# Recommendation scorer on one Trainium2 core: product of the sums and pooled copy one step later, pooling nine steps behind

## The chip, the cores and the metric

The kernel runs on one core of a Trainium2 chip (trn2). The metric is the device time of one execution in microseconds, taken as the median of several runs. A profile was taken of one further execution. TensorE is called PE here (its weight loads PEld), VectorE DVE, ScalarE ACT, GpSimd POOL and SyncE SP, as in the profile.

## The reference, cut to what matters

All tensors are float32, indices int32. There are B = 16384 samples with F = 69 user fields each, and a table `emb` of 100001 rows of E = 96.

```
u  = emb[batch_user]            # B x 69 x 96: 1,130,496 gathered rows
ql = emb[batch_label[:, 0]]     # B x 96
q  = ql broadcast over the 69 fields
z  = concat(q, u, q - u, q * u)
h  = dice(z @ W1 + b1, a1)      # 64 wide; dice: p = sigmoid(x*s), (a*(1-p) + p) * x
att = (h @ W2 + b2) @ W3 + b3   # one number for each sample and field
pre = where(batch_user < 100000, u * att, 0)
pooled = einsum('gf,bfe->bge', window, pre)     # 10 groups of fields
x = concat(pooled.reshape(B, 960), ql)
h = dice(x @ Wf1 + bf1); h = dice(h @ Wf2 + bf2); return h @ Wf3 + bf3
```

## The kernel before, in words

**Tiles and steps.** The samples are cut into 32 blocks of 512. A chunk is 512 pairs of sample and field: 64 chunks of a block hold 8 samples with 64 fields each, and 5 more ("tails") hold one of the last five fields for all 512 samples. So there are 69 chunks a block, 2208 in all, and a step `i` works on the two chunks `2i` and `2i+1`: 1104 steps and one closing step.

**What one pair of chunks goes through.** Seven pieces of work, written by seven functions:

1. `fetch(i)`: POOL gathers four times 128 rows a chunk into the buffer `u` (pool `upool`, 14 buffers); PE transposes them into PSUM (`ptr`, two buffers); DVE copies them to `uT` and multiplies them by the sample's own row to `quT`.
2. `hidden(i)`: PE forms the 64 sums of both chunks in PSUM (`ph`, pool `ps_h`, two banks); ACT takes the sigmoid into `y`; DVE makes the product of the sums and the gate in two instructions (L406 and L407) and leaves it in `y`.
3. `attend_rows(b, 4)`, once for four steps: PE reduces four `y` to a band `prow`, ACT copies it to `row`.
4. `spread(b, 4)`: PE transposes the band to `patt`, DVE turns it into the weights `rw` (two instructions, L436).
5. `pool(i)`: PE multiplies the gathered rows `u` by the weights `rw` into `acc`, eight matmuls as written (one for each quarter of a chunk; the trace has two records for each); DVE copies `acc` to `pooled` (L470). `ps_acc` has one buffer.
6. `attend_tail(i, j)`: the same for a tail chunk, through `pa` and `pre`.
7. `top1`, `top2`, `top3`: the three last layers of a block, spread over ten steps after the block's end.

**A quarter of some chunks comes another way.** For 109 chunks SP, and for 136 chunks ACT, fetch one quarter row by row: 128 DMAs of 384 bytes into the SBUF tensor `ring` (four buffers for SP, three for ACT), issued at L301 with addresses loaded at L286. SP issues a chunk's 128 in a row. ACT issues 16 in each step (`scalar_rows(i)`), in its own queue between the sigmoids.

**What sets the order.** The program is recorded with `tc.manual_schedule()`: nothing reorders it. A dictionary `plan` has for each step a list of pieces, filled by `at(step, ...)`, and each engine gets its instructions in that order. [...] In step `i` the order is: rows of the band that ends at `i-3` (where `i % 4 == 2`), tails of `i-3`, spread of the band (where `i % 4 == 3`), `hidden(i-2)`, ACT's 16 row DMAs, `pool(i-7)` (`POOL_LAG = 7`), `fetch(i)`, then pieces of the last layers. So DVE's own order in a step is: weights if it is their turn, product of `i-2`, pooled copy of `i-7`, `uT` and `quT` of `i`. PE's order is: rows, spread, sums of `i-2`, pooling of `i-7`, transposes of `i`. The last sixteen steps have an order of their own.

**Buffers and who frees them.** A gather buffer `u` is freed by PE's pooling of that step. The `acc` buffer is freed by DVE's pooled copy, the `ph` bank by DVE's product, the `ptr` buffer by DVE's `quT`.

Of the kernel before, what the change touches and what calls it, by code (L numbers as in the profile page):

```python
# [11 lines left out]
F32 = mybir.dt.float32  # L12
# [7 lines left out]
B, F, E, G = 16384, 69, 96, 10  # L20
# [9 lines left out]
NS = BLK // FM  # L30
# [7 lines left out]
S_BN = float(1.0 / np.sqrt(1.0 + 1e-5))  # L38


POOL_LAG = 7

NIDS = 4

# [2 lines left out]
CLOSE = 8  # L47
# [10 lines left out]
SINGLES = SP_CHUNKS + ACT_CHUNKS  # L58
NSB = (len(SINGLES) + P - 1) // P
NSEM = 8  # L60


def chunk_of(c):

    n, k = divmod(c, NCH)
    if n == NBLK - 1 and k >= EARLY:
        k = NMAIN + k - EARLY if k < EARLY + NTAIL else k - NTAIL
    return n, k
# [47 lines left out]
def rec_kernel(  # L116
# [12 lines left out]
    nc = tc.nc  # L129
# [1 line left out]

    const = ctx.enter_context(tc.tile_pool(name="const", bufs=1))
    ipool = ctx.enter_context(tc.tile_pool(name="ipool", bufs=2))
    upool = ctx.enter_context(tc.tile_pool(name="upool", bufs=14))
    tpool = ctx.enter_context(tc.tile_pool(name="tpool", bufs=4))
    ypool = ctx.enter_context(tc.tile_pool(name="ypool", bufs=6))
    rpool = ctx.enter_context(tc.tile_pool(name="rpool", bufs=2))
    bpool = ctx.enter_context(tc.tile_pool(name="bpool", bufs=2))
    xpool = ctx.enter_context(tc.tile_pool(name="xpool", bufs=1))
# [110 lines left out]
    ps_h = ctx.enter_context(tc.tile_pool(name="ps_h", bufs=2, space=PSUM))  # L250
    ps_x = ctx.enter_context(tc.tile_pool(name="ps_x", bufs=2, space=PSUM))
    ps_acc = ctx.enter_context(tc.tile_pool(name="ps_acc", bufs=1, space=PSUM))
    ps_m = ctx.enter_context(tc.tile_pool(name="ps_m", bufs=1, space=PSUM))


# [19 lines left out]
    class Singles:  # L275

        def __init__(self, name, engine, kind, chunks, first, buffers, group):
            self.name, self.engine, self.kind, self.group = name, engine, kind, group
            self.chunks, self.first, self.buffers = chunks, first, buffers
            self.sems = [tc.alloc_semaphore(f"{name}{k}") for k in range(NSEM)]  # L280
            self.given = [0] * NSEM

# [106 lines left out]
    def hidden(i, uT, quT):  # L389

        ph = ps_h.tile([P, 512], F32, tag="h", name=f"ph{i}")
        places = [chunk_of(2 * i + j) for j in range(2)]
        sums = [ph[j * H1 : (j + 1) * H1, :] for j in range(2)]
        for (n, k), p in zip(places, sums):
            if k >= NMAIN:
                nc.tensor.matmul(p, Cq, qTs[n % 2], start=True, stop=False)
        for j, ((n, k), p) in enumerate(zip(places, sums)):
            if k < NMAIN:
                nc.tensor.matmul(p, As[n % 2][:, k // 4, :], uT[j], start=True, stop=False)  # L399
            else:  # L400
                nc.tensor.matmul(p, A, uT[j][0:E], start=False, stop=False)
        for j, p in enumerate(sums):
            nc.tensor.matmul(p, Wp, quT[:, j, :], start=False, stop=True)  # L403
        y = ypool.tile([P, 512], F32, tag="y", name=f"y{i}")
        nc.scalar.activation(y, ph, AF.Sigmoid, scale=S_DICE)  # L405
        nc.vector.scalar_tensor_tensor(y, y, na1c, ph, ALU.mult, ALU.mult)  # L406
        nc.vector.scalar_tensor_tensor(y, ph, a1c, y, ALU.mult, ALU.add)  # L407
        return y

    def attend_rows(b, n):  # L410

# [11 lines left out]
        nc.tensor.matmul(pa, vrep[j * H1 : (j + 1) * H1, :], y[j * H1 : (j + 1) * H1, :], start=True, stop=True)  # L423
        nc.vector.scalar_tensor_tensor(pres[n][:, k - NMAIN, :], pa, bb[0:E], uT[j][0:E], ALU.add, ALU.mult)  # L424

    def spread(b, n):

        row = bands.pop(b)
        pt = ps_x.tile([P, 4, n, 32], F32, tag="x", name=f"patt{b}")
        for t in range(4):  # L430
            nc.tensor.transpose(  # L431
                pt[:, t].rearrange("p k j -> p (k j)"), row[:, t * P : (t + 1) * P], ident[0 : 32 * n, 0 : 32 * n]
            )
        rw = rpool.tile([P, 16, 2, 2 * G], F32, tag="rw", name=f"rw{b}")[:, 0 : 4 * n]
        for j in range(2):
            nc.vector.scalar_tensor_tensor(  # L436
                rw[:, :, j, :],
                pt.rearrange("p t k j -> p (t k) j")[:, :, j : j + 1].to_broadcast([P, 4 * n, 2 * G]),
                bb,
                R.rearrange("p (o g) -> p o g", o=1).to_broadcast([P, 4 * n, 2 * G]),  # L440
                ALU.add,
                ALU.mult,
            )
        for k in range(n):
            rws[b + k] = rw[:, k::n]
            ys.pop(b + k)

    def pool(i):

        u, rw = us.pop(i), rws.pop(i)  # L450
        todo = [(j, *chunk_of(2 * i + j)) for j in range(2)]
        todo = [(j, n, k) for j, n, k in todo if k < NMAIN]
        if not todo:
            return
        pa = ps_acc.tile([E, 2, NS, G], F32, tag="acc", name=f"acc{i}")
        for j, n, k in todo:
            for t in range(4):
                read_rows(
                    nc.tensor.matmul,
                    pa[:, j, 2 * t : 2 * t + 2, :].rearrange("e n g -> e (n g)"),  # L460
                    u,
                    2 * i + j,
                    t,
                    rw[:, t, j, :],
                    start=True,
                    stop=True,
                )
        if len(todo) == 2:
            _, n, k = todo[0]
            nc.vector.tensor_copy(  # L470
                pooled[n][:, :, k * NS : (k + 2) * NS].rearrange("e g s -> e s g"),
                pa.rearrange("e j s g -> e (j s) g"),
            )
        else:
            j, n, k = todo[0]
            nc.vector.tensor_copy(
                pooled[n][:, :, k * NS : (k + 1) * NS].rearrange("e g s -> e s g"), pa[:, j]
            )
# [58 lines left out]
        nc.vector.tensor_scalar(r, p3, bf3c[0:1], None, ALU.add)  # L537
        nc.sync.dma_start(out=out[B - P :].rearrange("p o -> o p"), in_=r)

    pooled, pres, x1s, x2s, qs, us, hs, ys, bands, rws, p1s = ({} for _ in range(11))  # L540

    def top_steps(n, cols):

# [14 lines left out]
    def rows_of(b, n):  # L558
        return lambda: attend_rows(b, n)

    def spread_of(b, n):
        return lambda: spread(b, n)

    def pool_of(k):
        return lambda: pool(k)

    def hidden_of(k):
        return lambda: ys.__setitem__(k, hidden(k, *hs[k]))

    def tails_of(k):  # L570
        def work():
            uT = hs.pop(k)[0]
            for j in range(2):
                if chunk_of(2 * k + j)[1] >= NMAIN:
                    attend_tail(k, j, ys[k], uT)

        return work

    def fetch_of(k, between=()):
        def work():  # L580
            for j in range(2):
                n = chunk_of(2 * k + j)[0]
                if n not in pooled:
                    pooled[n] = bpool.tile([E, G, BLK], F32, tag="pooled", name=f"pooled{n}")
                    pres[n] = xpool.tile([E, NTAIL, BLK], F32, tag="pre", name=f"pre{n}")
            u, uT, quT = fetch(k, lambda: [w() for w in between])
            us[k], hs[k] = u, (uT, quT)

        return work
# [4 lines left out]
    def at(step, *work):  # L594
        plan.setdefault(step, []).extend(work)
# [19 lines left out]
    def scalar_rows(i):  # L615

        for s, start, stop in turn.get(i, []):
            by_scalar.fetch(s, start, stop)

    c = NPAIR - CLOSE  # L620
    for i in range(c):
        if i >= 3 and (i - 3) % 4 == 3:
            at(i, rows_of(i - 6, 4))
        if i >= 3:
            at(i, tails_of(i - 3))
        if i >= 4 and (i - 4) % 4 == 3:
            at(i, spread_of(i - 7, 4))
        if i >= 2:
            at(i, hidden_of(i - 2))
        at(i, lambda i=i: scalar_rows(i))  # L630
        if i < c - CLOSE:
            if i >= POOL_LAG:
                at(i, pool_of(i - POOL_LAG))
        else:

            for k in {0: (-15, -14), 1: (-13,), 3: (-12, -11), 4: (-10, -9), 7: (-8, -7)}.get(i - c + 8, ()):
                at(i, pool_of(c + k))
        at(i, fetch_of(i))

    at(c, pool_of(c - 6), pool_of(c - 5), tails_of(c - 3), hidden_of(c - 2), fetch_of(c))  # L640
# [8 lines left out]
    for n in range(NBLK):  # L649
        first, end = n * NCH // 2, ((n + 1) * NCH - 1) // 2  # L650
        if n > 0:
            if n % NIDS == 1:
                at(max(0, first - 50), lambda n=n: load_ids(n))
            at(first - 14, lambda n=n: qs.__setitem__(n, head_gather(n)))
            at(first - 11, lambda n=n: head_turn(n, qs.pop(n)))
            at(first - 9, lambda n=n: head_rows(n))
        if n < NBLK - 2:
            for s, work in enumerate(top_steps(n, slice(0, BLK))):
                at(end + POOL_LAG + 4 + s, work)
        elif n == NBLK - 2:  # L660
            for s, work in enumerate(top_steps(n, slice(0, BLK))):
                at(end + POOL_LAG + s // 2, work)
    for f in range(NTAIL):
        at(2 + 2 * f, lambda f=f: tail_weights(f))

# [89 lines left out]
```

## Time and profile before

| | |
|---|---|
| time, median of 3 runs | 13698.38 us (13690.1 to 13716.8) |
| the profiled execution's own time | 13662.58 us, its span 13660.8 us |
| mean granted TensorE clock | 0.723 of full speed |
| PE busy | 9255.3 us, 68% of the span |
| POOL busy | 8237.3 us, 60% |
| DVE busy | 5106.9 us, 37% |
| ACT busy, its DMA issuing not counted | 992.1 us, 7% |
| row DMAs issued by ACT, by SP | 17408 and 13952 |
| gathers issued by POOL | 8715 |

The span is the time from the first instruction of the profiled execution to its last. Busy time of an engine is the union of its instructions; issuing a DMA and waiting for a semaphore don't count for ACT and SP, so an ACT that is full of issues looks idle. A group of section 5 of the page gives busy time, mean duration of one in nanoseconds, and the engine's idle time just before its instructions; "issue" and "remote" there mean that the profile shows no instruction that ended the wait. Some matmul records are missing from the trace, and then the wait for them shows as "remote". The profiled execution lies 0.26% below the median of the runs.

### The profile page before, as it was taken

The page shows a single profiled execution, that of the slowest core. Times are in us where ns is not written, and L with a number is a line of the kernel's source. Part 1 is how long each engine was busy: PE and PEld are TensorE (multiplying, and loading weights), DVE is VectorE, ACT ScalarE, POOL GpSimd, SP SyncE. Part 2 cuts the span into 40 slices and gives each one's busy share as a digit, 9 for nine tenths or more (in the row PEclk, how much of TensorE's full clock was granted, in tenths as well). Part 3 has the DMA queues.
Part 4 walks back from the last instruction along what each step waited for, and adds up shares of the span by engine and source line. Part 5 has one row for each costly group of instructions (what it writes and reads, how often), then busy time and mean ns, then how long its engine had stood idle before and what let it go on. Part 6 is the DMA issues. An engine that isn't in the chain of part 4 may idle for free.

```text
span 13660.8 us, 171082 instructions
## 1 busy us (share of the span) xinstructions
PE 9255.3 (68%) x41797; PEld 4797.0 (35%) x41797; DVE 5106.9 (37%) x8639; ACT 992.1 (7%) x1657; POOL 8237.3 (60%) x8721
## 2 busy tenths in 40 slices
PE   3667766667666776666776666666677666667667
PEld 2333333333333333333333333333333333333334
DVE  3333333333333333333433333333333333333333
ACT  0000000000000000000000000000000000000001
POOL 5665666565565656666666666665665666666664
PEclk7667777767766777777777777676777777777777
DMA  1111111111111111111111111111111111111111
GB/s 38 34 34 33 35 34 34 33 36 33 33 34 32 36 33 33 33 33 35 34 33 33 33 35 33 33 33 33 36 34 33 34 33 35 34 34 34 33 33 23
DMA packets 344459, 458.45 MB, mean 34 GB/s; under 512 B 202354, under 2 KB 202866, under 8 KB 343330
## 3 DMA queue, kind: packets, MB, share of 16 engines
q0 software_dynamic: 278880, 428.92, 15.8%
q1 hardware_dynamic: 29762, 11.82, 0.4%
q10 hardware_dynamic: 34816, 6.75, 0.3%
q8 instruction: 336, 5.51, 0.2%
q14 instruction: 665, 5.45, 0.1%
HBM read 446.74 MB, written 0.07 MB: 33 GB/s over the span
## 4 chain that ended last, share of the span: by engine, by line
PE 28%; issue 25%; ACTq 21%; another core or an unknown queue 14%; DVE 10%; ACT 2%; POOL 1%; DMA 0%; POOLq 0%
ACTq L301 18%; PE acc L325 6%; PE ptr L325 5%; PE ph L399 4%; PE p L502 4%; PE ph L403 4%; ACTq L286 2%; DVE uT L376 2%; DVE quT L379 2%; PE prow L414 2%; DVE y L406 2%; DVE y L407 2%; ACT y L405 1%; DVE pooled L470 1%
## 5 line engine op out<-in xcount | busy, mean ns | idle before, releaser
L266 POOL DMA_INDIRECT u<-in_rows,ids x8587 | 8115.1, 945 | 5284.9 <-issue 2284.1
L325 PE MATMUL acc<-rw,u 128*96 128x20 f32 x15930 | 2014.5, 272 | 1908.8 <-issue 1280.6
L325 PEld LDWEIGHTS acc<-rw,u 128*96 128x96 f32 x15930 | 1897.3, 205 | 2981.6 <-issue 2047.5
L406 DVE SCALAR_TENSOR_TENSOR y<-y,na1c,ph 128x512 f32<-128x512 f32 x1104 | 822.7, 745 | 4219.3 <-issue 2329.2
L325 PE MATMUL ptr<-ident,u 128*96 128x128 f32 x8587 | 1706.4, 350 | 718.5 <-issue 526.8
L376 DVE COPY uT<-ptr 96x512 f32<-96x512 f32 x2208 | 1485.5, 673 | 794.1 <-remote 619.1
L403 PE MATMUL ph<-quT,wn 96*64 96x512 f32 x4416 | 1611.4, 720 | 202.7 <-issue 196.4
L399 PE MATMUL ph<-uT,A 128*64 128x512 f32 x4096 | 1645.1, 830 | 82.0 <-issue 78.5
L325 PEld LDWEIGHTS ptr<-ident,u 128*96 128x96 f32 x8587 | 1284.6, 170 | 937.9 <-issue 701.2
L470 DVE COPY pooled<-acc 96x160 f32<-96x160 f32 x1008 | 424.7, 421 | 2693.5 <-remote 2166.1
L379 DVE TENSOR_TENSOR quT<-ptr,qT 96x512 f32<-96x512 f32 x2048 | 1378.9, 673 | 0.0
L405 ACT ACTIVATE y<-ph 128x512 f32<-128x512 f32 x1104 | 658.9, 597 | 8332.7 <-remote 3222.0
L403 PEld LDWEIGHTS ph<-quT,wn 96*64 96x64 f32 x4416 | 447.0, 175 | 1277.5 <-issue 1275.0
L407 DVE SCALAR_TENSOR_TENSOR y<-ph,wn,y 128x512 f32<-128x512 f32 x1104 | 829.1, 751 | 39.0
L414 PE MATMUL prow<-y,v 128*32 128x512 f32 x2208 | 645.9, 840 | 249.1 <-DVE y L407 133.0
L502 PE MATMUL p<-pooled,wf 96*100 96x512 f32 (+1 forms) x1400 | 701.0, 634 | 65.7 <-issue 61.6
L399 PEld LDWEIGHTS ph<-uT,A 128*64 128x64 f32 x4096 | 281.5, 170 | 753.7 <-issue 750.9
L502 PE MATMUL p<-pre,V 96*100 96x512 f32 (+1 forms) x700 | 423.9, 750 | 156.2 <-issue 107.4
L431 PE MATMUL patt<-ident,row 128*128 128x128 f32 x1108 | 257.0, 367 | 387.2 <-issue 205.8
L502 PEld LDWEIGHTS p<-pooled,wf 96*100 96x100 f32 x1400 | 249.4, 191 | 424.6 <-issue 424.0
L423 PE MATMUL pa<-y,vrep 64*96 64x512 f32 x320 | 189.8, 973 | 268.7 <-DVE pre L424 152.0
L416 ACT COPY row<-prow 128x512 f32<-128x512 f32 (+1 forms) x277 | 162.0, 585 | 2890.0 <-remote 1120.7
(72 smaller groups left out, 2729.4 us busy)
## 6 DMA issues: line engine op xcount, KB each, us to landing
ring<-in_rows ACTq DMA_DIRECT2D x17408, 0.4 KB
ring<-in_rows SPq DMA_DIRECT2D x13952, 0.4 KB
u<-in_rows,ids POOLq DMA_INDIRECT x8587
ids<-in_idx SPq DMA_DIRECT2D x8, 560.0 KB
q<-in_emb,ids POOLq DMA_INDIRECT x128
wf<-in_far SPq DMA_DIRECT2D x1, 1209.0 KB
wn<-in_near SPq DMA_DIRECT2D x1, 236.0 KB
ids<-in_idx SPq DMA_DIRECT2D x1, 140.0 KB
```

Source lines behind the costliest of these rows:

```text
L266: nc.gpsimd.indirect_dma_start(out=dst, out_offset=None, in_=table, in_offset=bass.IndirectOffsetOnAxis(ap=index, axis=0),)
L301: d = self.engine.dma_start(out=ring[r : r + 1, b], in_=row_bytes[:, bass.ds(self.values[r], ROW_BYTES)]).then_inc(self.sems[k], 16)
L325: ins = op(out, ring[:, at[0]].bitcast(F32) if at else u[:, 4 * (c % 2) + t, :], other, **how)
L376: nc.vector.tensor_copy(uT[j][0:E], ptr)
L379: nc.vector.tensor_tensor(quT[:, j, :].rearrange("e (s f) -> e s f", f=FM), ptr.rearrange("e (s f) -> e s f", f=FM), by_field(q[:, k * NS ...
L399: nc.tensor.matmul(p, As[n % 2][:, k // 4, :], uT[j], start=True, stop=False)
L403: nc.tensor.matmul(p, Wp, quT[:, j, :], start=False, stop=True)
L405: nc.scalar.activation(y, ph, AF.Sigmoid, scale=S_DICE)
L406: nc.vector.scalar_tensor_tensor(y, y, na1c, ph, ALU.mult, ALU.mult)
L407: nc.vector.scalar_tensor_tensor(y, ph, a1c, y, ALU.mult, ALU.add)
L414: nc.tensor.matmul(pr[32 * k : 32 * (k + 1), :], v2, ys[b + k], start=True, stop=True)
L502: nc.tensor.matmul(p1, w[:, h * DH : (h + 1) * DH], x, start=(k == 0), stop=(k == KTOP - 1))
```

## The change

`hidden` is cut into its sums with the sigmoid (`sums_of`) and DVE's product (`product`), `pool` into PE's matmuls (`pool_sums`) and DVE's copy (`pool_copy`), `spread` into PE's transposes (`turn_band`) and DVE's weights (`weigh`). In the main loop, which now ends sixteen steps before the last one's place (`e`), the DVE halves stand one step after the PE halves: the product of `i-3` instead of `i-2`, the copy of `i-10` beside the sums of `i-9`. `POOL_LAG` goes from 7 to 9. The one `acc` tile holds three sets of pooled sums side by side[...], set `i % 3` in turn. `upool` has 17 buffers instead of 14, `ypool` 7 instead of 6; to make room in SBUF the software DMA's scratch is set to 4096 bytes a partition. In the main loop the tails stand a step later, and the rows and the spread are put as the diff shows. The steps that lead to the end are written out anew, and the last layers of the last but one block start a step later than the new lag alone would have it.

```diff
-POOL_LAG = 7
+POOL_LAG = 9
+RING_BYTES = 4096
-    upool = ctx.enter_context(tc.tile_pool(name="upool", bufs=14))
+    upool = ctx.enter_context(tc.tile_pool(name="upool", bufs=17))
-    ypool = ctx.enter_context(tc.tile_pool(name="ypool", bufs=6))
+    ypool = ctx.enter_context(tc.tile_pool(name="ypool", bufs=7))
+    acc = ps_acc.tile([E, 3, 2, NS, G], F32, tag="acc", name="acc")
...
         nc.scalar.activation(y, ph, AF.Sigmoid, scale=S_DICE)
+        gates[i] = ph
+        ys[i] = y
+
+    def product(i):
+
+        ph, y = gates.pop(i), ys[i]
         nc.vector.scalar_tensor_tensor(y, y, na1c, ph, ALU.mult, ALU.mult)
         nc.vector.scalar_tensor_tensor(y, ph, a1c, y, ALU.mult, ALU.add)
-        return y
...
-        pa = ps_acc.tile([E, 2, NS, G], F32, tag="acc", name=f"acc{i}")
+        pa = acc[:, i % 3]
...
+        accs[i] = pa, todo
+
+    def pool_copy(i):
+
+        if i not in accs:
+            return
+        pa, todo = accs.pop(i)
...
     c = NPAIR - CLOSE
-    for i in range(c):
-        if i >= 3 and (i - 3) % 4 == 3:
-            at(i, rows_of(i - 6, 4))
-        if i >= 3:
-            at(i, tails_of(i - 3))
-        if i >= 4 and (i - 4) % 4 == 3:
-            at(i, spread_of(i - 7, 4))
-        if i >= 2:
-            at(i, hidden_of(i - 2))
-        at(i, lambda i=i: scalar_rows(i))
-        if i < c - CLOSE:
-            if i >= POOL_LAG:
-                at(i, pool_of(i - POOL_LAG))
-        else:
...
+    e = c - CLOSE
+    for i in range(e):
+        if i >= 7 and i % 4 == 3 and i < e - 1:
+            at(i, rows_of(i - 7, 4))
+        if i >= 4:
+            at(i, tails_of(i - 4))
+        if i >= 8 and i % 4 == 0:
+            at(i, lambda b=i - 8: turn_band(b, 4))
+        if i >= 2:
+            at(i, sums_of(i - 2))
+        at(i, lambda i=i: scalar_rows(i))
+        pools = [] if i < POOL_LAG else [i - POOL_LAG]
+        if i == e - 2:
+            pools.append(i - POOL_LAG + 1)
+        elif i == e - 1:
+            pools = [i - POOL_LAG + 1]
+        at(i, *[lambda k=k: pool_sums(k) for k in pools])
+        if i >= 3:
+            at(i, product_of(i - 3))
+        at(i, *[lambda k=k: pool_copy(k) for k in ([] if i <= POOL_LAG else [i - POOL_LAG - 1, i - POOL_LAG][: 1 + (i == e - 1)])])
...
+        at(i, fetch_of(i))
+        if i >= 8 and i % 4 == 0:
+            at(i, lambda b=i - 8: weigh(b, 4))
...
+    for i in range(e, c):
...
+        at(i, hidden_of(i - 2), lambda i=i: scalar_rows(i))
+        for k in {0: (-16, -15), 1: (-14,), 2: (-13,), 3: (-12, -11), 4: (-10, -9), 7: (-8, -7)}.get(i - e, ()):
+            at(i, pool_of(c + k))
         at(i, fetch_of(i))
...
-                at(end + POOL_LAG + s // 2, work)
+                at(end + POOL_LAG + 1 + s // 2, work)
...
-    nc = bacc.Bacc("TRN2", target_bir_lowering=False, num_devices=1)
+    nc = bacc.Bacc("TRN2", target_bir_lowering=False, num_devices=1, dynamic_dma_scratch_size=RING_BYTES)
```

More of the change, by code (lines that the diff above doesn't have):

```diff
@@ L424, in attend_tail, with turn_band @@
         nc.vector.scalar_tensor_tensor(pres[n][:, k - NMAIN, :], pa, bb[0:E], uT[j][0:E], ALU.add, ALU.mult)
-    def spread(b, n):
+    def turn_band(b, n):
         row = bands.pop(b)
@@ L433, in spread, with weigh @@
             )
+        turned[b] = pt
+    def weigh(b, n):
+        pt = turned.pop(b)
         rw = rpool.tile([P, 16, 2, 2 * G], F32, tag="rw", name=f"rw{b}")[:, 0 : 4 * n]
@@ L446, in spread, with pool_sums @@
             ys.pop(b + k)
-    def pool(i):
+    def pool_sums(i):
         u, rw = us.pop(i), rws.pop(i)
@@ L538, in top3_last @@
         nc.sync.dma_start(out=out[B - P :].rearrange("p o -> o p"), in_=r)
-    pooled, pres, x1s, x2s, qs, us, hs, ys, bands, rws, p1s = ({} for _ in range(11))
+    pooled, pres, x1s, x2s, qs, us, hs, ys, bands, rws, p1s, gates, turned, accs = ({} for _ in range(14))
     def top_steps(n, cols):
@@ L561, in spread_of, with work, sums_of, product_of @@
     def spread_of(b, n):
-        return lambda: spread(b, n)
+        def work():
+            turn_band(b, n)
+            weigh(b, n)
+        return work
     def pool_of(k):
-        return lambda: pool(k)
+        def work():
+            pool_sums(k)
+            pool_copy(k)
+        return work
     def hidden_of(k):
-        return lambda: ys.__setitem__(k, hidden(k, *hs[k]))
+        def work():
+            hidden(k, *hs[k])
+            product(k)
+        return work
+    def sums_of(k):
+        return lambda: hidden(k, *hs[k])
+    def product_of(k):
+        return lambda: product(k)
     def tails_of(k):
@@ L620, in rec_kernel @@
     c = NPAIR - CLOSE
-    for i in range(c):
-        if i >= 3 and (i - 3) % 4 == 3:
+    e = c - CLOSE
[18 more added lines that the diff above has]
+        at(i, *[lambda k=k: pool_copy(k) for k in ([] if i <= POOL_LAG else [i - POOL_LAG - 1, i - POOL_LAG][: 1 + (i == e - 1)])])
+        if i == e - 2:
+            at(i, rows_of(c - 16, 4))
+        elif i == e - 1:
+            at(i, lambda: turn_band(c - 16, 4))
+        at(i, fetch_of(i))
+        if i >= 8 and i % 4 == 0:
+            at(i, lambda b=i - 8: weigh(b, 4))
+        elif i == e - 1:
+            at(i, lambda: weigh(c - 16, 4))
+    at(e, product_of(e - 3), lambda: pool_copy(e - POOL_LAG), tails_of(e - 4))
+    for i in range(e, c):
+        if (i - 3) % 4 == 3:
             at(i, rows_of(i - 6, 4))
-        if i >= 3:
-            at(i, tails_of(i - 3))
-        if i >= 4 and (i - 4) % 4 == 3:
+        at(i, tails_of(i - 3))
+        if (i - 4) % 4 == 3:
             at(i, spread_of(i - 7, 4))
-        if i >= 2:
-            at(i, hidden_of(i - 2))
-        at(i, lambda i=i: scalar_rows(i))
-        if i < c - CLOSE:
-            if i >= POOL_LAG:
-                at(i, pool_of(i - POOL_LAG))
-        else:
-            for k in {0: (-15, -14), 1: (-13,), 3: (-12, -11), 4: (-10, -9), 7: (-8, -7)}.get(i - c + 8, ()):
-                at(i, pool_of(c + k))
+        at(i, hidden_of(i - 2), lambda i=i: scalar_rows(i))
+        for k in {0: (-16, -15), 1: (-14,), 2: (-13,), 3: (-12, -11), 4: (-10, -9), 7: (-8, -7)}.get(i - e, ()):
+            at(i, pool_of(c + k))
         at(i, fetch_of(i))
```

## The prediction

> **What bounds the kernel now.** I read the busy shares first, then the groups with their idle time, then the timeline of a few steps, then the clock by windows. Section 1 of the page:
>
> ```profile
> span 13660.8 us, 171082 instructions
> ...
> PE 9255.3 (68%) x41797; PEld 4797.0 (35%) x41797; DVE 5106.9 (37%) x8639; ACT 992.1 (7%) x1657; POOL 8237.3 (60%) x8721
> ```
>
> No engine is full: a step is 12.37 us (13660.8 / 1104), PE is busy for 8.4 of it. So something makes them wait for each other. Section 5 says where (after the bar: busy us, mean ns, idle before):
>
> ```profile
> L266 POOL DMA_INDIRECT u<-in_rows,ids x8587 | 8115.1, 945 | 5284.9 <-issue 2284.1
> L325 PE MATMUL acc<-rw,u 128*96 128x20 f32 x15930 | 2014.5, 272 | 1908.8 <-issue 1280.6
> ...
> L406 DVE SCALAR_TENSOR_TENSOR y<-y,na1c,ph 128x512 f32<-128x512 f32 x1104 | 822.7, 745 | 4219.3 <-issue 2329.2
> L325 PE MATMUL ptr<-ident,u 128*96 128x128 f32 x8587 | 1706.4, 350 | 718.5 <-issue 526.8
> ...
> L470 DVE COPY pooled<-acc 96x160 f32<-96x160 f32 x1008 | 424.7, 421 | 2693.5 <-remote 2166.1
> ```
>
> PE's idle time stands mostly before `acc`, DVE's before the product (L406) and the copy (L470). The timeline shows the link between them:
>
> ```profile
> 6239.41 10.26 ACTq L301 DMA_DIRECT2D ring<-in_rows  x16
> ...
> 6247.48 1.03 PE L403 MATMUL ph<-quT,wn 96*64 96x512 f32 x4
> ...
> 6249.77 0.60 ACT L405 ACTIVATE y<-ph 128x512 f32<-128x512 f32 x1 [12.04 <-PE ph L403]
> 6249.84 10.46 ACTq L301 DMA_DIRECT2D ring<-in_rows  x16
> 6250.40 0.75 DVE L406 SCALAR_TENSOR_TENSOR y<-y,na1c,ph 128x512 f32<-128x512 f32 x1 [8.45 <-ACT y L405]
> ...
> 6251.18 0.75 DVE L407 SCALAR_TENSOR_TENSOR y<-ph,wn,y 128x512 f32<-128x512 f32 x1
> 6251.85 0.41 DVE L470 COPY pooled<-acc 96x160 f32<-96x160 f32 x1
> ...
> 6252.32 1.77 PE L325 MATMUL acc<-rw,u 128*96 128x20 f32 x16 [3.81 <-issue]
> ```
>
> PE ends its sums at 6248.5 and stands still for 3.81 us. It needs the one `acc` buffer, which the copy frees at 6252.26. The copy stands behind the product, the product waits for the sigmoid, and the sigmoid stands in ACT's queue behind sixteen row DMAs (6239.41 + 10.26 = 6249.67; sigmoid at 6249.77). So ACT's issuing stops PE through DVE's queue. In other steps it is the reverse: ACT is done with its DMAs and waits for PE's sums. Going through all 1104 sigmoids, 53% start within 0.3 us of the end of ACT's earlier work, and 30% come over 2 us after it. PE and ACT take turns in holding each other up.
>
> The clock makes it worse (columns: busy of PE, PEld, DVE, ACT, POOL, then the granted clock):
>
> ```profile
> 6180.00:6190.00 10.00, 10.00 (x52) 5.20 (x50) 4.14 (x7) 0.60 (x1) 5.97 (x7) 1.00 0.15 30
> 6340.00:6350.00 10.00, 1.33 (x5) 0.51 (x5) 1.82 (x3) 0.60 (x1) 7.56 (x8) 0.50 0.21 40
> ```
>
> [...]
>
> Gathers do not bound: the first `uT` copy of a step starts 76 us or more after its gather was issued (99% of steps). POOL has filled the 14 buffers and waits for PE.
>
> [...] the clock's records are 1.0 or 0.5 only, in pieces that are multiples of 3.41 us, 0.723 in the mean. [...] The trace shows 278880 packets for 8715 gathers, 32 each[...].
>
> **The change, part by part.** As built, both programs have the same 25933 matmuls, 8636 DVE operations, 8715 gathers and 31374 DMAs of ACT and SP; PE gets 70 more pure wait instructions, a few us at most. So only order and waits move.
>
> *Product one step later.* In step i DVE does the product of i-3. Its sigmoid was queued a step earlier. In the built program, PE's transposes of i wait for `quT` of i-1 as before, but that stands behind the product of i-4, no longer i-3. Removed: most of the 718.5 us before `ptr`.
>
> *Copy one step later, three sets.* The pooling of i waits for the copy that DVE does in step i-1, as before; it is not three sets of freedom[...]. But that copy stands behind the product of i-4 instead of i-3. The weights of a band are now made a step before their first use; before, PE's `acc` waited for them some 500 us. Removed: most of the 1908.8 us before `acc`.
>
> *New wait.* With two `ph` banks and the product a step later, PE's sums of i-2 wait for the product of i-4, done by DVE in step i-1. Behind them in PE's queue stand the pooling of i-9 and the transposes of i; ACT waits for those sums. Bounds: nothing where ACT is ahead, and where ACT is late up to all that was removed. `patt` still waits for ACT's band copy of the step before (387.2 us now); a PE that runs further ahead waits longer there, once in four steps.
>
> *Gather buffers and lag.* A buffer lives 9 steps instead of 7, and there are 17: POOL may lead PE by 8 steps instead of 7. POOL's order is unchanged. Its own time is 8715 x (0.945 + 0.30) = about 10,890 us, so it has some 2770 us to spare. Rows in `ring` are freed two steps later; ACT's buffer is rewritten 14 steps after its transposes and read by the pooling 9 after them instead of 7, so ACT gets no wait. SP's refill starts two steps later, with over 20 steps to spare. Cost nothing; without that cover it would be SP's 128 issues, about 100 us a chunk.
>
> *Descriptor scratch.* Nothing in the trace of before prices it. [...] I take 0. From the other side, it decides nothing until a gather costs 1.57 us instead of 1.25 (13661 / 8715).
>
> *Ends.* First poolings two steps later, sixteen last steps rearranged: plus or minus 20 us; I take 0.
>
> **The sum.** ACT is the engine to count. Its DMA pieces add up over the trace to about 9600 us (0.55 us each), the address loads to 544 x 2.16 = 1175, what else is not under DMAs to 300: 11,075. So it is idle for about 2585 us, 1960 of them before sigmoids. How much of this goes? For each sigmoid that waited I took the smaller of ACT's wait and PE's idle time before `acc` and `ptr` since the sigmoid before, and since the one before that: 630 and 1120 us in all. These are waits that PE would not have caused had it not stood still itself. The change moves the limit by one step, so I take 1000. A less interrupted PE has a higher clock: 0.75 for 0.723 takes 3.6% off 9255 us, 330, half of it where PE is the late one: 155. Against it: next to a gather in progress ACT's issues are 0.59 us apart, with none 0.39. With POOL at 86% instead of 80% that is 0.011 x 17408 = 190, of which 110 where ACT is the late one. Sum: 13,662 - 1000 - 155 + 110 = 12,617. The median of the runs is 0.26% above the profiled execution: 12,650.
>
> **The rivals.**
>
> *A, as summed (0.52):* 12,650, itself from 12,250 to 13,150.
>
> *B, decoupled fully (0.22).* PE always has a step in hand and stays at the full clock; ACT sets the pace with POOL nearly full behind it: 11,075 + 0.035 x 17408 (issues at 0.585 us) = 11,680, with some 200 us at band copies and ends 11,900. For it: with the clock at 1.00 (6230 to 6240 us) a step's sums came 7.7 us after the last ones. Against: `patt` and the last layers still tie PE and DVE to the end of ACT's queue.
>
> *C, the wait only changes its name (0.14).* It stands before `ph` and `patt` instead of `acc`: only the 500 us at the weights go, and a third of that shows: 13,500. For it: the same sigmoid still precedes all. Some of this case lies within 0.2%.
>
> *D, slower (0.12): the clock.* If PE's waits gather into fewer, longer ones (at `patt`, up to one batch of ACT's DMAs, 8 to 10 us, every fourth step), more windows fall to half clock. At 0.5 throughout PE alone needs 9255 x 0.723 / 0.5 = 13,380, with 1000 us of waits left 14,400. It decides from a mean clock of about 0.58 on: 9255 x 0.723 / 0.58 = 11,540, and the 2160 us of PE's idle time that stand neither before `acc` nor `ptr` fill the rest. Against it: fewer waits in all.
>
> **How the numbers follow.** A measurement tells about 0.2% from no change (27 us). Faster: A, B and three quarters of C, 0.84; same: a quarter of C, 0.04; slower 0.12. The range leaves out D and the lower part of B: 11,850 to 13,720. A's own is 12,250 to 13,150.
>
> **What would show it.** Right: the idle time before `acc` falls from 1908.8 to under 800 us and before `ptr` from 718.5 to under 400; a new group of waits before `ph`, under 600; the mean clock at 0.74 or more; the product no longer starts 0.03 us after its sigmoid but finds it done. POOL's idle time falls with the span. Wrong: as much idle time before `ph` and `patt` as was taken away (C), a clock under 0.6 (D), a gather group with mean over 945 ns or new gaps between gathers (the scratch), ACT idle under 500 us (B).

## The result and the profile after

The changed kernel takes 13684.62 us (median of 12 runs, 13673.53 to 13723.87), the kernel before 13698.64 us (12 runs). The ratio is 0.9994, with a 95% interval from 0.9983 to 1.0004: no change that a measurement can tell. The forecast was 12,650 us. One thing has to be known to read what follows: in some of the later groups of runs (a group is run together on one chip) the kernel before took 13,507 to 13,657 us, near the 13,699 on record, in others 10,928 to 10,947 us, and two chips had both; so each run below is set against the kernel before of its own group. I call the first kind **stalled** and the second **free**, for a reason that the traces show. The result itself is stalled.

The page of the changed kernel, sections 1 and 5 (after the bar: busy us, mean ns of one, idle us before and what ended most of it):

```profile
span 13682.6 us, 171148 instructions
...
PE 9106.3 (67%) x41797; PEld 4711.6 (34%) x41797; DVE 5074.9 (37%) x8639; ACT 990.6 (7%) x1657; POOL 8225.3 (60%) x8721
...
L268 POOL DMA_INDIRECT u<-in_rows,ids x8587 | 8103.5, 944 | 5290.9 <-issue 2228.3
L327 PE MATMUL acc<-rw,u 128*96 128x20 f32 x15930 | 1972.9, 269 | 1685.7 <-issue 1088.5
L489 DVE COPY pooled<-acc 96x160 f32<-96x160 f32 x1008 | 429.0, 426 | 6575.4 <-remote 4728.2
...
L327 PE MATMUL ptr<-ident,u 128*96 128x128 f32 x8587 | 1655.6, 341 | 866.1 <-issue 659.3
...
L414 DVE SCALAR_TENSOR_TENSOR y<-y,na1c,ph 128x512 f32<-128x512 f32 x1104 | 810.3, 734 | 177.1 <-ACT y L407 97.0
```

The change did what it says on DVE: the product waited 4219.3 us before, now 177.1. But DVE then waits at the pooled copy (2693.5 before, 6575.4 now). PE's idle time hardly moved: before `acc` 1908.8 to 1685.7, before `ptr` 718.5 to 866.1. And POOL's row is the same to 6 us in its idle time.

That row leads to the cause. In both traces POOL's gathers come as strings, 1.249 us from one to the next, and between strings there is a stop, at nine steps in ten. Before: 979 stops over 0.6 us, median 2.35 us, 2962 us in all. After: 978 stops, median 2.39 us, 2970 us in all. For the kernel before, 8715 x 1.249 = 10,885 us of gathers and 2962 - 979 x 0.30 = 2668 us that the stops add (0.30 us is the gap between two gathers of a string) give 13,553; its last gather ends at 13,563 us of 13,661. Such a sum comes out for any engine; that each gather counts in full, stops or not, is shown by e15 below. A string is one step's gathers, 7 or 8 of them, in 850 of 978 cases before and in 849 of 977 after: three more gather buffers did not make it longer.

What happens in a string and at its end is seen in the timeline of the changed kernel (start, duration, engine; in brackets the idle time before). The usual case:

```profile
6384.47 1.53 PE L327 MATMUL acc<-rw,u 128*96 128x20 f32 x16
...
6385.85 1.06 PE L327 MATMUL ptr<-ident,u 128*96 128x128 f32 x8
...
6387.75 1.03 PE L405 MATMUL ph<-quT,wn 96*64 96x512 f32 x4
...
6388.87 0.94 POOL L268 DMA_INDIRECT u<-in_rows,ids  x1 [0.30 <-issue]
6391.82 0.42 DVE L489 COPY pooled<-acc 96x160 f32<-96x160 f32 x1 [7.74 <-remote]
6392.06 0.94 POOL L268 DMA_INDIRECT u<-in_rows,ids  x1 [2.24 <-remote]
6392.10 0.66 DVE L378 COPY uT<-ptr 96x512 f32<-96x512 f32 x1
```

PE has pooled by 6386.00, transposed by 6386.91 and summed by 6388.78, and the string's last gather ends at 6389.81. Yet DVE, with nothing else to do for 7.74 us, copies the pooled sums only at 6391.82 and the transposes at 6392.10, and POOL goes on at 6392.06. Nobody acts on PE's finished work until 2 us after the string.

Counts over the whole trace say the same. 11,358 of PE's instructions in it raise a semaphore, a counter that the other engines' instructions wait for. In e17, the kernel before in a free group, 98% of these instructions are followed by a recorded increment within 0.1 us (median 14 ns). In the trace of the changed kernel only 18% are (median 3.2 us; 9% of the increments have no record, so this is a lower bound). Of the recorded increments 81% fall between the end of a string and the restart after it, where only 19% of the raising instructions end. The first of them comes 2.03 us after the string's end in the median, and POOL restarts 0.02 us after one of them, while the last pooling had ended 6.4 us before. The kernel before shows the same (17% within 0.1 us, 80% between string and restart, 2.01 us, pooling 6.2 us earlier).

The rarer case is a PE that crawls itself:

```profile
6634.23 0.32 PE L327 MATMUL acc<-rw,u 128*96 128x20 f32 x1 [1.09 <-issue]
...
6635.68 0.32 PE L327 MATMUL acc<-rw,u 128*96 128x20 f32 x1 [1.14 <-issue]
...
6636.94 0.95 POOL L268 DMA_INDIRECT u<-in_rows,ids  x1 [0.30 <-issue]
6637.79 0.19 PE L327 MATMUL acc<-rw,u 128*96 128x20 f32 x1 [1.79 <-issue]
...
6639.20 0.19 PE L327 MATMUL acc<-rw,u 128*96 128x20 f32 x1 [1.23 <-issue]
...
6639.93 0.80 PE L327 MATMUL acc<-rw,u 128*96 128x20 f32 x4 [0.54 <-issue]
...
6641.01 0.94 POOL L268 DMA_INDIRECT u<-in_rows,ids  x1 [3.12 <-PE ptr L327]
```

Pooling matmuls of one step come here one at a time, 0.7 to 2.1 us apart, though the profile shows nothing that they wait for. The last four follow 2 us after the string's last gather ended (6637.89), and POOL restarts 0.28 us after them. Only 13% of the 978 restarts follow the last pooling within 0.5 us. Of PE's 1695 us of idle time before pooling matmuls, those on `ring` included, 1401 us stand before the first one of a step and 294 us between them.

So POOL waits for PE, as the prediction said, but mostly for word of work that PE has already done. Most of the `acc` group's idle time, "issue" included, stands where a step's pooling has to wait for DVE, and crawl between the matmuls is the smaller part. DVE hears from PE mostly once a string, with the old order of its own work as with the new (80% and 81% of the recorded increments). This fits a change that gained nothing, but no run changed when PE's word arrives.

### The profile page after: what moved, and what is told of

It reads as the page before. It is cut to its first block, busy times and chain, and to the rows that moved or that the text cites. A ratio compares the mean times of both kernels' runs of the same rounds, so it can differ in the third digit from the quotient of the medians.

```text
span 13682.6 us, 171148 instructions
## 1 busy us (share of the span) xinstructions
PE 9106.3 (67%) x41797; PEld 4711.6 (34%) x41797; DVE 5074.9 (37%) x8639; ACT 990.6 (7%) x1657; POOL 8225.3 (60%) x8721
## 4 chain that ended last, share of the span: by engine, by line
PE 37%; issue 20%; another core or an unknown queue 18%; ACTq 12%; DVE 10%; POOL 2%; ACT 1%; DMA 0%; POOLq 0%
ACTq L303 10%; PE acc L327 8%; PE ph L401 6%; PE ptr L327 6%; PE ph L405 5%; PE p L521 5%; DVE uT L378 3%; DVE quT L381 2%; POOL u L268 2%; PE prow L421 2%; DVE y L415 1%; DVE y L414 1%; ACTq L288 1%; PE pa L430 1%
## 5 line engine op out<-in xcount | busy, mean ns | idle before, releaser
L327 PE MATMUL acc<-rw,u 128*96 128x20 f32 x15930 | 1972.9, 269 | 1685.7 <-issue 1088.5
L489 DVE COPY pooled<-acc 96x160 f32<-96x160 f32 x1008 | 429.0, 426 | 6575.4 <-remote 4728.2
L327 PEld LDWEIGHTS acc<-rw,u 128*96 128x96 f32 x15930 | 1853.6, 201 | 2757.0 <-issue 1954.3
L327 PE MATMUL ptr<-ident,u 128*96 128x128 f32 x8587 | 1655.6, 341 | 866.1 <-issue 659.3
L405 PE MATMUL ph<-quT,wn 96*64 96x512 f32 x4416 | 1625.1, 727 | 195.2 <-issue 189.6
L401 PE MATMUL ph<-uT,A 128*64 128x512 f32 x4096 | 1637.7, 830 | 156.9 <-issue 106.2
L327 PEld LDWEIGHTS ptr<-ident,u 128*96 128x96 f32 x8587 | 1250.6, 166 | 1082.2 <-issue 864.1
L414 DVE SCALAR_TENSOR_TENSOR y<-y,na1c,ph 128x512 f32<-128x512 f32 x1104 | 810.3, 734 | 177.1 <-ACT y L407 97.0
L438 PE MATMUL patt<-ident,row 128*128 128x128 f32 x1108 | 259.5, 375 | 641.4 <-issue 274.9
L421 PE MATMUL prow<-y,v 128*32 128x512 f32 x2208 | 540.7, 851 | 115.0 <-issue 95.6
L438 PEld LDWEIGHTS patt<-ident,row 128*128 128x128 f32 x1108 | 185.1, 194 | 775.8 <-issue 554.0
L430 PE MATMUL pa<-y,vrep 64*96 64x512 f32 x320 | 231.3, 895 | 203.2 <-DVE pre L431 127.6
```

The source lines that it names most:

```text
L327: ins = op(out, ring[:, at[0]].bitcast(F32) if at else u[:, 4 * (c % 2) + t, :], other, **how)
L421: nc.tensor.matmul(pr[32 * k : 32 * (k + 1), :], v2, ys[b + k], start=True, stop=True)
```

## The experiments

Theories: **G**, gathers set the pace; **A**, ACT's string of row transfers sets it, as the prediction counted; **P**, PE at its clock; **R**, in the stalled groups the time follows the number of instructions and of transfers that complete, an assumption of the author's from the crawl and the missing records (counted under "What is settled, what is open"). All kernels are the changed one with an edit, but for e17. The texts written before the runs speak of two kinds of chip; the runs corrected that, chips 3 and 10 were seen in both conditions. e5, e9, e12, e14, e16 and e18 are several executions each, the others one; within a group the executions of the kernel before lie within 0.6% of each other.

### Gathers, ACT's rows, all rows, PE's work (e1 to e4; a free group, kernel before 10,946.5 us)

```
e1:  -                else:
     +                elif (j, t) != (0, 0):     # one gather less per step
e2:  ACT_CHUNKS = []
e3:  ACT_CHUNKS = []; SP_CHUNKS = [17]
e4:  - nc.tensor.matmul(p, Wp, quT[:, j, :], start=False, stop=True)
```

> The changed kernel with one gather of 128 rows per step left out: tile 0 of a step's first chunk is not fetched, its readers read tile 1's rows instead, so the output differs; all other work is there. Theory G (POOL's string of gathers sets the pace: n gathers at 1.25 us and about 2.2 us of release per step): 1104 x 1.25 = 1,380 us less, about 12,300 us. Theory A (ACT's string of row transfers sets it, as the prediction counted): ACT issues the same transfers; at most the share of them that ran beside the missing gather becomes quicker, about 1/8 of (0.61 - 0.44) us x 17,408 = 370 us less, about 13,300 us. Theory P (TensorE at its granted clock): no change, about 13,680 us.

> The changed kernel with ACT's 17,408 row transfers taken out; their 136 chunk tiles are fetched by 136 more gathers on POOL. Theory G: 136 x 1.25 = 170 us more, about 13,850 us. Theory A: ACT is left with sigmoids and copies, some 1,500 us of work, so the time falls to the next bound, between 11,000 us (POOL's 8,851 gathers at 1.245 us) and 12,500 us. Theory P: no change, 13,680 us.

> The changed kernel with the row transfers of both ACT and SP taken out (one chunk is left on SP); 244 more gathers on POOL do their work. Theory G: 244 x 1.25 = 305 us more, about 13,990 us. Theory A: as without ACT's rows, 11,000 to 12,600 us. If the two strings of row transfers slow the gathers or the release of POOL (the 2.2 us per step), this run is faster than the one in which only ACT's are out by more than SP's 108 added gathers cost it (135 us).

> The changed kernel without the 4,416 matmuls that add the second product to the sums (ph from quT); the output differs, every transfer and every other instruction stays. Theory P (TensorE sets the pace): its 1,611 us of busy time go, about 12,100 us. Theory G: TensorE releases POOL earlier by what it saves only if it is itself late; between no change (13,680) and 12,900 us. Theory A: no change, 13,680 us.

Measured: e1 9602.81 us, e2 11,116.58, e3 11,227.22, e4 10,930.76. Without 1104 gathers the time falls by 1344 us, 1.22 each; with 136 more it rises by 170, 1.25 each; with 244 more by 281, 1.15 each. 17,408 row transfers less on ACT, or 4416 matmuls less on PE, bring nothing. In these traces POOL has no stop over 0.6 us at all. For the free groups G stands, A and P fall. e2 and e4 were not run in a stalled group. The absolute figures of the expectations were for a stalled group.

### The change itself (e5, stalled; e9, free)

The edit is the change.

> The changed kernel as it is, beside the kernel before on one chip. In the group of four looks the kernel before took 10,946 us where the runs on record have 13,699 us, and in them POOL never stopped between gathers (8,715 x 1.25 = 10,894 us). Theory G2 (that chip runs both kernels at POOL's own pace of one gather per 1.25 us): here, if this chip is of that kind, both kernels take about 10,945 us and the ratio is 1.00 within 0.002, since the change neither adds nor removes a gather. If this chip is of the other kind, both take about 13,690 us and the ratio is again 0.999. Theory L (the change removes waits that count only where POOL has reserve to give): on the quick kind of chip the lead of three more buffers shows as a gain, at most the 50 us that 10,946 us has over 8,715 gathers. Against both: a difference over 1%.

> The changed kernel as it is, on the chip of the three looks before it. On a chip of the quick kind (the kernel before at 10,946 us): POOL never stops, 8,715 x 1.25 = 10,894 us; the change can give back only what lies around that, so a ratio between 0.995 and 1.001. On a chip of the slow kind: as before, between 0.998 and 1.001 by theory R, since the number of instructions and of completions is the same in both kernels.

Measured: e5 13,500.68 us against 13,510.80, ratio 0.9992 (0.9985 to 0.9999); e9 10,937.86 against 10,934.39, ratio 1.0004 (0.9995 to 1.0013). Neither condition gains: in e5 the interval leaves 1.00 by a hair, far inside what counts here as no change.

### All rows and a gather out again, and idle memsets (e6 to e8, free)

```
e7:  + filler = const.tile([P, 1], F32, name="filler")
     ... after each quT:                 for _ in range(8):  nc.vector.memset(filler, 0.0)
     ... after the product's second op:  for _ in range(16): nc.vector.memset(filler, 0.0)
```

> The same kernel as e3 (no row transfers by ACT and SP but those of one chunk; 244 more gathers), for a chip on which the kernel before takes about 13,500 to 13,700 us. On that kind of chip five sixths of the records of the gathers' completions are missing from the trace (some 2,700 of 17,400 for each of their eight semaphores), and matmuls, row transfers and VectorE's operations that wait for nothing come at multiples of 0.7 us while gathers run. Theory R (there [...]time follows the number of instructions; 63,500 of 171,100 go here): POOL's own pace becomes the bound, about 11,230 us. Theory G (gathers alone hold the others up, 2.2 us a step): 244 x 1.25 = 305 us more than 13,500 to 13,700. Theory A (ACT's own string of transfers): 11,200 to 12,600 us. On a chip of the quick kind: 11,230 us by all.

> The changed kernel with 32 VectorE memsets of one element per partition added to each step, 35,328 in all, that nothing reads; VectorE is idle for more than half of the time. Theory R, on a chip of the slow kind: a fifth more instructions, so up to a fifth more of the time, between 14,300 and 16,000 us. Theories G and A: VectorE gets some 35,328 x 0.06 = 2,100 us more of work beside its 5,100 in 13,500: no change, at most 150 us for products that come later. On a chip of the quick kind: POOL stays the bound, 10,930 to 11,000 us by all.

> The same kernel as e1 (one gather of 128 rows per step left out), for a chip of the slow kind. Theory G (n gathers at 1.25 us and 2.2 us of release per step): 1,380 us less than the kernel before. Theory R: the instructions are nearly the same (1,104 of 171,100 less) but an eighth of the gathers' completions goes: between 300 and 1,700 us less. Theory A: at most 370 us less. On a chip of the quick kind: about 9,600 us as in e1.

Measured, kernel before 10,934.39 us: e6 11,233.00, e7 10,989.28, e8 9583.96, as expected for a free group. They could not tell R from the others; 35,328 memsets cost 55 us there.

### Idle memsets for a stalled group (e10, e11 free; e13 stalled)

The edit is that of e7.

> The kernel of e7 (35,328 idle memsets on VectorE), sent for a chip on which the kernel before takes 13,500 to 13,700 us. Theory R[...]: a fifth more instructions, between 14,300 and 16,000 us. Theories G (gathers alone) and A (ACT's string of transfers): no change, at most 150 us. On a chip of the quick kind: about 10,990 us as in e7.

> The kernel of e7 and e10 (35,328 idle memsets on VectorE) once more, for a chip on which the kernel before takes 13,500 to 13,700 us. Theory R: between 14,300 and 16,000 us. Theories G and A: no change, at most 150 us. On a chip of the quick kind: about 10,990 us.

> The kernel of e7 (35,328 idle memsets on VectorE), for a chip on which the kernel before takes 13,500 to 13,700 us. Theory R: between 14,300 and 16,000 us. Theories G and A: no change, at most 150 us. On a chip of the quick kind: about 10,990 us as in e7.

Measured: e10 10,987.31 us against 10,928.05 and e11 10,993.05 against 10,929.92; both groups were free, so they add nothing to e7. e13: 14,223.10 against 13,529.23, 694 us more, 20 ns for each memset that nothing reads. Section 5 of its page:

```profile
L268 POOL DMA_INDIRECT u<-in_rows,ids x8587 | 8103.9, 944 | 5793.0 <-issue 2207.0
L365 DVE MEMSET filler<- 128x1 f32 x35328 | 2084.4, 59 | 5632.4 <-DVE filler L365 3366.5
```

The second row shows memsets that wait on their own predecessor, 3366.5 us of it (in e7 the row has 2018.7 us of idle time in all, none of it in gaps over 0.15 us): DVE crawls too. POOL's stops come to 3481 us, against 2781 in e5: the 700 us are there. By G alone and by A at most 150 us should have been lost, so instructions do cost something as such; R had the sign but its 14,300 to 16,000 us was too high.

### No rows, one gather less, for a stalled group (e14, e15)

The edits are those of e3 and e1; kernel before 13,657.44 us.

> The kernel of e3 (no row transfers but those of one chunk; 244 more gathers), for a chip of the slow kind (kernel before 13,500 to 13,700 us). Theory R: 63,500 of 171,100 instructions go; at the 20 ns that an idle memset cost there that alone is 1,250 us[...], so between 11,230 us (POOL's own pace, 8,959 x 1.25 and ends) and 12,300 us. Theory G: 305 us more than the kernel before. Theory A: 11,230 to 12,600 us. On a chip of the quick kind: 11,230 us, a ratio of 1.027.

> The kernel of e1 (one gather of 128 rows per step left out), for a chip of the slow kind. Theory G: 1,380 us less than the kernel before. Theory R: an eighth of the gathers' completions goes, 300 to 1,700 us less. Theory A: at most 370 us less. On a chip of the quick kind: about 9,600 us.

Measured: e14 13,382.43 us, ratio 0.9797 (0.9781 to 0.9814); e15 12,232.24 us. A falls here too: with no rows at all on ACT it wanted 12,600 us or less. R in its strong form falls with it: 37% of the instructions are gone and the time is 2% less. What stays of R is small: a gather less per step saves 1425 us, 1.29 each (G: 1380), so the 244 gathers that e14 has more cost about 315, and its rows saved 275 + 315 = 590 us, 19 ns each, the price of a memset in e13. In e14 POOL still makes 610 stops, 2271 us in all; in e15 991, 2904 us. The stops stay when the rows are gone; with the rows, and more with the memsets, they come to more in all (2781 us in e5, 3481 in e13). Two limits: R had allowed 300 to 1700 us for e15, so e15 alone does not tell G from a form of R that counts the gathers' completions; and P was not tested by a stalled run. The kept trace speaks against P. In the kernel before, ten steps in a row that carry a block's last layers (50 or more of their matmul records) keep PE busy for 96 us, ten that carry none for 82 us, and yet they take 123.5 and 129.2 us; in the changed kernel it is 96 and 80 us, 122.4 and 129.1.

### More rows on SP (e12, e16, e18; all stalled)

```
- SP_CHUNKS = [2 * (10 * s + 8) + 1 for s in range(109)]
+ SP_CHUNKS = [2 * (6 * s + 8) + 1 for s in range(181)]
```

> The changed kernel with 72 more chunk tiles fetched row by row by SP (181 chunks, one in 6 steps, where it has 109, one in 10) and 72 gathers fewer on POOL. On a chip of the quick kind (kernel before about 10,930 us), where POOL never stops: 72 x 1.25 = 90 us less, a ratio of 0.992, unless SP's strings of 128 rows at 0.32 us become late (41 us and the loads of offsets per 6 steps of 9.9 us), then slower. On a chip of the slow kind (13,500 to 13,700 us): theory G 90 us less or a little more; theory A no change, ACT's string is the same; theory R 72 x 128 = 9,216 more transfers, with their instructions some 18,900 (11%) more, so 300 to 1,500 us more.

> The kernel of e12 (72 more chunk tiles fetched row by row by SP, 72 gathers fewer), for an occasion on which the kernel before takes about 10,930 us: 72 x 1.25 = 90 us less, a ratio of 0.992; it would be the quickest of all kernels here with complete work. If SP's strings come late (41 us of rows and the loads of offsets per 6 steps of 9.9 us), it is slower. On an occasion with 13,500 to 13,700 us for the kernel before: 1.16 as in e12.

> The kernel of e12 and e16 (72 more chunk tiles fetched row by row by SP, 72 gathers fewer). On an occasion on which the kernel before takes about 10,930 us: 72 x 1.25 = 90 us less, a ratio of 0.992, or slower if SP's strings come late. On one with 13,500 to 13,700 us: 1.16 as before.

Measured ratios: 1.1595 (1.1563 to 1.1628), 1.1589 (1.1555 to 1.1622), 1.1519 (1.1491 to 1.1548). That is more than any theory said. The chain of e12's page and its group of transposes that read the ring name the place:

```profile
SPq 61%; issue 37%; PE 1%; DVE 0%; another core or an unknown queue 0%; DMA 0%; ACT 0%; ACTq 0%
...
L327 PE MATMUL ptr<-ident,ring 128*96 128x128 f32 x317 | 118.9, 375 | 4035.9 <-DMA ring<-in_rows 3938.7
```

SP's queue is full: 23,168 rows at 0.67 us (mean of the spacings under 3 us, here and below) are 15,520 of 15,822 us. In the free trace e9 its rows come 0.386 us apart, in the stalled trace of before 0.804. The expectation had priced a row at 0.32 us; in the stalled groups it takes twice that and turns SP into the bound. Whether the move gains in a free group was not seen.

### The kernel before in a free group (e17)

> The kernel before itself, for its trace on an occasion on which it takes about 10,930 us. If the change did what the prediction says and POOL hides it, PE's idle time before acc is several hundred us here and DVE's product waits for the sigmoid (over 500 us), against 14.6 and 32.2 us in e9. If those waits came from the stalls alone, both are as small here as in e9. On an occasion with 13,500 to 13,700 us it repeats the profile on record: about 1,900 us before acc.

Measured: 10,929.90 us, as its neighbour. Its section 5 beside that of e9, first the kernel before, then the changed one:

```profile
L266 POOL DMA_INDIRECT u<-in_rows,ids x8587 | 8104.2, 944 | 2619.7 <-issue 2413.5
L325 PE MATMUL ptr<-ident,u 128*96 128x128 f32 x8587 | 2003.9, 333 | 1963.0 <-DMA u<-in_rows,ids 1914.0
L406 DVE SCALAR_TENSOR_TENSOR y<-y,na1c,ph 128x512 f32<-128x512 f32 x1104 | 824.6, 747 | 3371.0 <-ACT y L405 3311.6
...
L325 PE MATMUL acc<-rw,u 128*96 128x20 f32 x15930 | 1801.7, 259 | 43.0 <-DVE rw L436 31.2
...
L470 DVE COPY pooled<-acc 96x160 f32<-96x160 f32 x1008 | 419.2, 416 | 115.9 <-PE acc L325 115.7
```

```profile
L268 POOL DMA_INDIRECT u<-in_rows,ids x8587 | 8113.2, 945 | 2619.2 <-issue 2431.0
L327 PE MATMUL ptr<-ident,u 128*96 128x128 f32 x8587 | 1979.3, 333 | 1892.1 <-DMA u<-in_rows,ids 1869.4
...
L327 PE MATMUL acc<-rw,u 128*96 128x20 f32 x15930 | 1808.3, 259 | 14.6 <-DVE rw L448 8.1
L489 DVE COPY pooled<-acc 96x160 f32<-96x160 f32 x1008 | 430.3, 427 | 2826.2 <-PE acc L327 2772.4
...
L414 DVE SCALAR_TENSOR_TENSOR y<-y,na1c,ph 128x512 f32<-128x512 f32 x1104 | 810.7, 734 | 32.2 <-ACT y L407 32.2
```

Of the 1908.8 us before `acc` 43.0 are left in the very same program, and of the 1280.6 us "issue" nothing. So nearly all of that idle time came with the stalls. Of the two forecasts each is half right: the wait before `acc` is as small as in e9, DVE's wait for the sigmoid is not. PE's real wait is before `ptr`, and a gather's landing ends it: POOL's idle time is 8714 gaps of 0.30 us, nothing else. DVE's wait moves from product to copy here as well, and it costs and saves nothing.

### What is settled, what is open

Settled: in the free groups POOL's gathers set the time, 1.249 us each, without stops. In the stalled ones a gather left out counts in full as well (1.29 us, e15), and stops come on top, at nine steps in ten in the result's two traces, at 610 of 1104 in e14. The change alters neither the gathers nor the stops.

Open: what holds PE's increments back while gathers run, what makes single instructions crawl, and why a string is one step long. The stalled traces also lack most records of the gathers' completions: each of their eight semaphores has 2613 to 2746 records in the kernel before, and 17,254 to 17,341 in e9, for the same 8715 gathers. Engines that crawl, increments that come late and records that are missing are seen together here; no run shows that the one causes the other.

## Why the prediction was wrong

**The step that failed** is "Gathers do not bound" with "so it has some 2770 us to spare". The 10,890 us were right (10,885 measured). The 2770 us beside them were read as a reserve, since the transposes came 76 us after their gathers and POOL waited for PE. They were 979 stops, 2.35 us in the median, one after each of POOL's own strings, until word of PE's work came through. With a reserve, a gather less a step should save nothing; it saved 1425 us in the stalled e15 and 1344 in the free e1.

**"ACT is the engine to count"** fell with it. The sum took 0.55 us for a row issue as ACT's price; it is 0.345 us between rows in e17. ACT's rows could go altogether at no gain in a free group (e2), and in a stalled one ACT's and SP's together were worth 590 us, not the pace (e14).

**"Removed: most of the 1908.8 us before acc", "most of the 718.5 us before ptr".** 1685.7 and 866.1 us stayed. The timeline shown in the prediction, with 3.81 us before `acc`, was read as a queue through product and sigmoid; but its sigmoid (6249.77) also starts 0.24 us after POOL's restart from a stop of 2.29 us (6249.53), so it fits late word from PE as well. The free trace of the same program has 43.0 us in all. One instance was taken for the group. So the term of 1000 us was 0. The wait of `acc` for the weights, put at some 500 us and expected to go, is 274.5 us before by the trace (PE's waits for `rw`) and 504.0 after.

**The clock**: 0.75 was forecast, 0.72 came (0.723 before), so the 155 us were 0 too. The two stretches shown in the prediction are near the ends of a wide range: in the trace of before, the 117 stretches of 10 us in which PE is busy for 99% or more have a clock of 0.79 in the mean, the 121 with PE busy for under 30% one of 0.61. From one piece of 3.41 us to the next the tie is closer: all 756 pieces that follow one with PE busy for under 30% have 0.5, the 1554 that follow one with 95% or more have 0.895 in the mean. And PE's time does not go fully with the clock, as the 155 us and D's 13,380 us assume: a matmul of `quT` takes 594 ns at 1.0 and 1060 at 0.5, a transpose 276 and 421, a pooling matmul 240 and 325. **ACT's pace beside gathers**, 110 us lost, had no POOL speed-up to arise from.

**What was right.** The product no longer follows its sigmoid by 0.03 us; the median is 4.34 us. The wait before `ph` stays small, 156.9 and 195.2 us for its two groups (82.0 and 202.7 before) against the 600 us allowed for a new one. The longer wait at `patt` came, 387.2 to 641.4 us. The gathers keep their 944 ns (945 before), and no cost of the smaller scratch shows. Three sets in `acc` gave no freedom, as said: in neither trace does a pooling matmul run during any of the 1040 pooled copies.

**The rivals.** C ("the wait only changes its name") comes nearest with its 13,500 us, and the name did change on DVE; but its place was to be `ph` and `patt`, and the time was kept by POOL's strings and stops, not by ACT. B and D did not come. D's 2160 us of PE idle time are 1778 in the trace (13,660.8 - 9255.3 - 1908.8 - 718.5); nothing else rests on them. No rival had POOL's strings in it, and so no change was given a chance of only 0.04.

## What to carry to other kernels

Before an engine is called free, see where its waits lie. Here POOL's 2770 us of idle time were stops after its own strings, and a gather less still saved its full price. Take away one unit of what each engine does and see what the time does, before an order of queues is rebuilt. And before waits are read, look whether the semaphores' records are all there and follow the instructions that raise them: where they do not, "issue" and "remote" do not say that nothing was waited for, and one clear instance in a timeline is not the group.

## What the runs showed of the hardware

- The same program took 10,930 us and 13,650 us on the same chip (chips 3 and 10) at different times. Within a group it kept to one of them, within 0.6%.
- While a string of gathers runs in a stalled trace, PE's semaphore increments come late. In the nine stalled traces 17 to 30% of the raising instructions are followed by a record within 0.1 us, in the eleven free ones 97% or more. In the two stalled traces of the result some 80% of the records lie in the stop after a string, from about 2 us after its last gather on.
- In stalled traces ACT's row issues keep to steps: of some 17,400 in the kernel before, 10,541 come 0.3 to 0.4 us after the last, 1113 after 0.7 to 0.8, 1635 after 1.4 to 1.5, 579 after 2.1 to 2.2. In e17 nearly all, 15,531, lie in the first.
- A VectorE memset of one element per partition cost the whole kernel 20 ns in a stalled group and 1.6 to 1.8 ns in a free one.
- An edit need not have the same sign in both: with no rows on ACT and SP (e14, e6) the kernel takes 2.0% less time than the kernel before in a stalled group and 2.7% more in a free one.
